# First rows of a scan kernel by products over 128 partitions, scaled by whole-tile operations

## The chip, the cores and the metric

The kernel runs on one core of a Trainium2 chip. The metric is the time of one execution on the device in microseconds (us); a kernel's time is the median of its runs. The profile is one further execution, recorded by the hardware profiler.

## The reference

The input x has 32 images of 48 channels, 64 rows and 128 columns in f32. Two layers of the same kind follow each other. A layer normalises x per image in 16 groups of 3 channels, scans the result in four directions, and adds what comes out to x:

```python
def step(w, b):
    def f(carry, inp):
        nxt = inp + _conv1d(carry, w, b)   # 5 taps, 48 channels to 48
        return (nxt, nxt)
    return f
...
# down over the rows, up over the rows, right over the columns, left over the columns
x = x + _L0_conv_ref(_gn(x), L0_conv_down_w, ...)
x = x + _L1_conv_ref(_gn(x), L1_conv_down_w, ...)
```

Each scan step needs the result of the step before it, so the steps form one chain: 63 steps down and 63 up, then 127 right and 127 left.

## The kernel before, in words

**Tiling.** The images are worked on in four groups of 8. For a scan over rows, a row of a group is a tile of three parts (o = 0 to 2) with 128 partitions and 128 columns each: eight neighbouring image columns e times 48 channels fill 3 x 128 partitions, and the 128 columns are 16 blocks k of such eight columns times 8 images b. The table PIECES says which channels of which e lie on which partitions of which part. A step is 9 matrix products (PRODUCTS, L856), each recorded as two instructions, and three vector operations (L865) that add the bias and the input row to the sums and write the new row. The phases (PHASES) are 8 row phases (4 groups, 2 layers) of 126 steps and 4 column phases of 254 steps, one after the other. TensorE works through this chain; all else is planned beside it.

**Order.** Instructions are put in an order written by hand: the function in_order ties every instruction to the one before it on its engine, so each engine works in the order of the program, and waits there. The calls at(t, ...) put other work into an agenda by step number; it is issued before that step. first_group is the start-up, which is issued in full before step 1 of the first phase; then the steps and the agenda alternate.

**The start-up before.** In the order of the program:

- load_kernel and make_ident load the small weights and build a selection matrix in the still unused tile of the later left weights (wleft); place_kernel has TensorE spread the weights over the partitions (L1210), and ACT copies them out (L1213, L1214).
- The first eight rows of the group go to a tile `top` in their natural layout, rows 0 to 3 on partitions 0 to 47 and rows 4 to 7 on partitions 64 to 111, by one load on SP's queue and one on ACT's. The whole group follows in `parts`: 16 loads of 768 KB on SP's queue, in a layout of 128 partitions that each hold 24 rows of input.
- DVE takes the statistics of the parts (L485, L488).
- put_rows permutes one of these 24 input rows by four copies (L637) on POOL or ACT into a tile, and put_out writes the tile to DRAM (`xin`) through SP's queue. All 24 must be there before every image row can be loaded back in the scan's layout.
- rows_by_product makes image rows 0 to 7 without the way through DRAM: a product with a piece of the selection matrix (48 partitions, 512 columns, L1243) moves the channels of one e to their partitions, reading `top` with a stride over the images, and ACT copies the sums out (L1250). Six such groups of products are needed (two sets of four rows, three parts): four come before the coefficients, two after.
- scaling computes scale and offset of each image and channel from the statistics through small products (L363, L374), a square root on ACT (L405) and small DVE operations (last is L415).
- scale_first scales rows 0 to 3, one image and part at a time: 15 operations on DVE (L711), 9 on ACT (L713). scale_rows does the same on ACT for the following rows (L688, 24 operations per call).
- move_rows loads image rows back from `xin`, ten loads (pieces) per call on SP's queue: rows 8 to 11, rows 12 to 15, and then eight at a time. ACT scales rows up to 47; scale_at_once does rows 48 to 63 on POOL with two whole-tile operations (multiply, then add; L699).

The copies need tiles that are still free: parts of the rows 8 to 31 of the scan's own tile, of the later weights, and of `stage`; a tile is used again when its write to DRAM has landed. The product tiles in PSUM (`rows0` to `rows2`) exist once each, so a group of products waits until ACT has copied the group before it out of the same tile.

Of the kernel before, what the change touches and what calls it, by code (L numbers as in the profile page):

```python
# [29 lines left out]
F32 = mybir.dt.float32  # L30
# [3 lines left out]
C = 48  # L34
# [7 lines left out]
GB = 8  # L42
# [77 lines left out]
def kernel(  # L120
# [62 lines left out]
    mask_in = wt["left"].rearrange("p i n -> p (i n)")[:, 5 * FULL : 5 * FULL + NG * C]  # L183
# [496 lines left out]
    def scale_rows(k, h0, h1):  # L680
        _, layer, g = PHASES[k]
        scale, offset = coeffs[layer, g]
        view = row_views(k)[h0 // HALF][:, :, h0 % HALF : h0 % HALF + h1 - h0]
        view = view.rearrange("p o h (k b) -> p o b h k", b=GB)
        for b in range(GB):
            for o in range(NG):
                args = view[:, o, b], scale[:, o, b : b + 1], offset[:, o, b : b + 1]
                nc.scalar.activation(  # L688
                    args[0], args[0], AF.Identity, bias=args[2], scale=args[1]
                )  # L690

    def scale_at_once(k, h0, h1, eng):

        _, layer, g = PHASES[k]
        view = row_views(k)[h0 // HALF][:, :, h0 % HALF : h0 % HALF + h1 - h0]
        view = view.rearrange("p o h (k b) -> p o (h k) b", b=GB)
        for t, op in zip(coeffs[layer, g], (ALU.mult, ALU.add)):
            t = t.unsqueeze(2).to_broadcast([FULL, NG, (h1 - h0) * NK, GB])
            eng.tensor_tensor(view, view, t, op)  # L699

    def scale_first(k, h1, split):

        _, layer, g = PHASES[k]
        scale, offset = coeffs[layer, g]
        view = row_views(k)[0][:, :, 0:h1].rearrange("p o h (k b) -> p o b h k", b=GB)
        for b in range(GB):
            for o in range(NG):
                it = view[:, o, b]
                by, on = scale[:, o, b : b + 1], offset[:, o, b : b + 1]
                if b < split:  # L710
                    nc.vector.tensor_scalar(it, it, by, on, ALU.mult, ALU.add)  # L711
                else:
                    nc.scalar.activation(it, it, AF.Identity, bias=on, scale=by)  # L713
# [431 lines left out]
    def first_group():  # L1145
# [6 lines left out]
        whole = shift[:, 0 : 2 * FULL + start - C // 3 + ODD]  # L1152
        part = shift[:, whole.shape[-1] : whole.shape[-1] + FULL + ODD]
        SETS = ((0, C), (ODD, ODD + C))

        def selects(piece, s=0):
            e, c0, c1, o, p0 = piece
            t, at = (part, 0) if c0 and p0 else (whole, start - p0 + c0)
            p, q = SETS[s]
            return t[p:q, at + p : at + p + FULL]  # L1160

        rows = PR // 2
        four = E8 // 2
        top = stage[:, 0:2].rearrange("p i n -> p (i n)").rearrange("p (b m) -> p b m", b=GB)
        parts = [wide_nat(SLOT + i * SLOT, rows) for i in range(2)]
        stats = InputStats("x0", GB)
        n = W * GB

        kernel = slot[slots(0)[0]][0:C, 0 : TAPS * C + 6]
        zeros = slot[slots(0)[0]][0:C, 512 : 512 + NG * FULL + 6]  # L1170

        def load_kernel():
            nc.vector.memset(zeros, 0.0)
            for j in range(TAPS):
                d, si = divmod(TAPS - 1 - j, 2)
                to = kernel[:, j * C : (j + 1) * C]
                dma(to, w[SIDES[si], 0, DOWN, d, SIDES[0]], nc.scalar if j % 2 else nc.sync)
            aside(kernel[:, TAPS * C :], bias[0:C].rearrange("c l k -> c (l k)"))

        def make_ident():  # L1180
            nc.vector.memset(shift[:, 0 : whole.shape[-1] + FULL + ODD], 0.0)
            for t, base in ((whole, start), (part, 2 * C - C // 3)):
                nc.gpsimd.affine_select(
                    t,
                    t,
                    pattern=[[1, t.shape[-1]]],
                    compare_op=ALU.not_equal,
                    fill=1.0,
                    base=-base,
                    channel_multiplier=-1,  # L1190
                )
            nc.gpsimd.memset(part[:, 0 : 2 * C], 0.0)
            nc.gpsimd.memset(part[:, 2 * C - C // 3 + ODD : 2 * C + ODD], 0.0)

        def place_kernel():
            for i in range(NG):
                ps = ps_rows.tile([FULL, BN], F32, tag=f"rows{i}", name=f"rows{i}")
                todo = [(selects(PIECES[0]), zeros, slice(0, NG * FULL + 6))]
                for piece in PIECES:
                    e, c0, c1, o, p0 = piece  # L1200
                    if o == i:
                        m = selects(piece)
                        for run in WEIGHT_RUNS:
                            if run[0:4] == (c0, c1, i, p0):
                                _, _, _, _, at, to, n = run
                                todo.append((m, kernel[:, at : at + n], slice(to, to + n)))
                        tail = slice(NG * FULL, NG * FULL + 6)
                        todo.append((m, kernel[:, TAPS * C :], tail))
                for j, (lhs, rhs, to) in enumerate(todo):
                    nc.tensor.matmul(  # L1210
                        ps[:, to], lhs, rhs, start=j == 0, stop=j == len(todo) - 1
                    )
                nc.scalar.copy(wt["down0"][:, i], ps[:, 0 : NG * FULL])  # L1213
                nc.scalar.copy(  # L1214
                    bd[:, i].rearrange("p l k -> p (l k)"), ps[:, NG * FULL :][:, 0:6]
                )

        free = [
            row_views(0)[0][:, o, h : h + 8].rearrange("p h n -> p (h n)")
            for h in (8, 16, 24)  # L1220
            for o in range(NG)
        ]
        free += [early[:, WEIGHTS + i * n : WEIGHTS + (i + 1) * n] for i in range(3)]
        free += [stage[:, i // 2, i % 2 * n : (i % 2 + 1) * n] for i in range(4, 8)]
        order = [*range(0, 4), *range(8, 12), *range(4, 8), *range(16, 20)]
        order += [*range(12, 16), *range(20, 24)]
        tiles = free + free[3:]
        put = [0]

        def put_rows(*engines):  # L1230
            for eng in engines:
                r, perm = order[put[0]], tiles[put[0]]
                put[0] += 1
                permute(parts[r // rows], r % rows, perm, (eng,))
                put_out(0, r, perm)

        def rows_by_product(s, o):
            src = top[SETS[s][0] : SETS[s][1]]
            src = src.rearrange("p b (r k e) -> p e r k b", k=NK, e=E8)
            ps = ps_rows.tile([FULL, four * N], F32, tag=f"rows{o}", name=f"rows{o}_{s}")  # L1240
            mine = [piece for piece in PIECES if piece[3] == o]
            for i, piece in enumerate(mine):
                nc.tensor.matmul(  # L1243
                    ps.rearrange("p (r k b) -> p r k b", r=four, b=GB),
# [4 lines left out]
                )  # L1249
            nc.scalar.copy(  # L1250
                row_views(0)[0][:, o, s * four : (s + 1) * four],
                ps.rearrange("p (r n) -> p r n", n=N),
            )

        pool, act = nc.gpsimd, nc.scalar
        load_kernel()
        for s, (p0, p1) in enumerate(SETS):
            src = x[0:GB].rearrange("b c h w -> c b (h w)")
            dma(
                top[p0:p1],  # L1260
                src[:, :, s * four * W : (s + 1) * four * W],
                nc.scalar if s else nc.sync,
            )
        for i in range(2):
            for b in range(GB):
                dma(parts[i][:, b], flat(b)[:, i * rows * W : (i + 1) * rows * W])
# [3 lines left out]
        place_kernel()  # L1270
        make_masks()
        for b in range(GB):
            stats.take(0, parts[0], b)
        put_rows(pool, act, pool, act)
        rows_by_product(0, 0)
        put_rows(pool, act, pool, act)
        rows_by_product(0, 1)
        put_rows(pool, act, pool)
        rows_by_product(0, 2)
        put_rows(pool)  # L1280
        rows_by_product(1, 0)
# [3 lines left out]
        put_rows(act, pool)  # L1285
        for _ in scaling("x0", 0, 0, stats, x_masks):
            pass
        scale_first(0, 4, 5)
        put_rows(pool, act, pool, act)
        rows_by_product(1, 1)  # L1290
        rows_by_product(1, 2)
        move_rows(0, 8, 12, False)
        put_rows(pool, act, pool, pool, pool, pool)
        move_rows(0, 12, 16, False)
        scale_rows(0, 4, 8)
        scale_rows(0, 8, 12)
        scale_rows(0, 12, 16)
        for h in range(16, 64, 8):
            move_rows(0, h, h + 8, False)
            if h < 40:  # L1300
                scale_rows(0, h, h + 8)
        take_in(1, 0, nats1[0])

    in_order(first_group)
    at(starts[0] + 10, scale_rows, 0, 40, 48)
# [72 lines left out]
```

## Time and profile before

| what | value |
|---|---|
| runs of the kernel (median of 3; lowest, highest) | 4215.19 us (4209.02, 4222.83) |
| the profiled execution's own time | 4228.38 us |
| its span, first to last instruction | 4226.6 us |
| coefficients ready (end of L415) | 50.9 us |
| first matmul of step 1 | 62.27 us |
| statistics (L485) begin, their last result (L488) begins | 12.41, 43.94 us |
| POOL's copies of rows begin and end (L637) | 25.7, 62.2 us |
| loads of rows 12 and on are issued from | 82.2 us |

Times in the tables and lines count from the first instruction. A line of the page's groups reads: source line, engine, operation, what it writes from what it reads, shapes, count, then the busy time and the mean duration of one in ns, and last the idle time of the engine just before it with what ended it. A line of the timeline reads: start, duration, engine, source line, operation, operands, count of merged instructions, and in brackets the idle time before it with its cause. PEld is TensorE's loading of a stationary matrix, which overlaps its products. Mean durations of single instructions overlap their neighbours; the spacing of a run of them is what they cost.

### The profile page before, as it was taken

To read this page: it belongs to the slowest core of one execution; us is meant where nothing else is said; L and a number is where in the kernel's file an instruction comes from. 1 tells how busy PE (TensorE), PEld (TensorE's weight loads), DVE (VectorE), ACT (ScalarE), POOL (GpSimd) and SP (SyncE) were. 2 spreads that over 40 slices of the span, in tenths; PEclk is the share of its full clock that TensorE was granted. 3 is DMA by queue.
4 is the path that set the end of the run, shared out by engine and by line. 5 is a ranking of instruction groups with operands and counts; after the bars stand their busy time and mean duration, and the time that the engine had idled before them with its cause. 6 is when DMAs were issued, how large, how long until landed. Compare 5 with 4: busy or idle time off the path is not lost. (4 is left out here: it accounts for less than half of the span.)

```text
span 4226.6 us, 90155 instructions
## 1 busy us (share of the span) xinstructions
PE 4086.4 (97%) x36724; PEld 4055.0 (96%) x36724; DVE 2135.8 (51%) x6501; ACT 1287.5 (30%) x2525; POOL 791.2 (19%) x737
## 2 busy tenths in 40 slices
PE   8999999999999999999999999999999999999992
PEld 6999999999999999989999999999999999999992
DVE  5454444456644454444457654444444444444443
ACT  6844000536874633000016854503000012110122
POOL 3520010334322100010023310000000034410352
PEclk9999999999999999999999999999999999999996
DMA  9987669659979997259419979759188059899999
GB/s 293 236 174 115 110 126 209 216 148 250 208 187 172 199 151 126 41 102 202 84 48 265 203 144 156 114 80 161 32 147 182 1 99 246 236 260 156 177 202 182
DMA packets 2118431, 680.55 MB, mean 161 GB/s; under 512 B 2006416, under 2 KB 2056832, under 8 KB 2079616
## 3 DMA queue, kind: packets, MB, share of 16 engines
q1 hardware_dynamic: 2015504, 582.07, 69.0%
q10 hardware_dynamic: 99952, 87.20, 9.7%
q0 software_dynamic: 2560, 5.51, 0.5%
q8 instruction: 289, 4.73, 0.5%
q14 instruction: 126, 1.03, 0.1%
HBM read 397.77 MB, written 295.14 MB: 164 GB/s over the span
## 5 line engine op out<-in xcount | busy, mean ns | idle before, releaser
L688 ACT ACTIVATE arena<-arena,offset,scale 128x256 f32<-128x256 f32 (+2 forms) x840 | 582.3, 788 | 310.4 <-DMA arena<-mid 176.8
L788 POOL TENSOR_TENSOR arena<-arena 128x2048 f32<-128x2048 f32 x80 | 362.9, 4548 | 1442.6 <-PE step_10l L856 461.4
L637 POOL COPY arena<-arena 128x256 f32<-128x256 f32 x332 | 196.7, 660 | 443.1 <-DMA arena<-in_x 394.2
L575 ACT ACTIVATE early<-arena 128x256 f32<-128x256 f32 x192 | 129.5, 674 | 453.6 <-DMA arena<-xin 315.2
L856 PE MATMUL step_01r<-arena,early 128*128 128x128 f32 x2286 | 254.2, 275 | 10.0 <-DMA arena<-arena 5.4
L856 PEld LDWEIGHTS step_01r<-arena,early 128*128 128x128 f32 x2286 | 253.3, 187 | 10.9 <-DVE arena L865 6.0
L856 PE MATMUL step_00r<-arena,early 128*128 128x128 f32 x2286 | 253.5, 275 | 8.7 <-DMA arena<-arena 4.4
L856 PEld LDWEIGHTS step_00r<-arena,early 128*128 128x128 f32 x2286 | 252.8, 186 | 9.4 <-issue 4.8
L856 PE MATMUL step_11r<-arena,early 128*128 128x128 f32 x2286 | 251.5, 274 | 5.5 <-DVE arena L865 5.5
L856 PEld LDWEIGHTS step_11r<-arena,early 128*128 128x128 f32 x2286 | 251.0, 185 | 5.9 <-DVE arena L865 5.8
L856 PE MATMUL step_00l<-arena,wleft 128*128 128x128 f32 x2286 | 249.3, 272 | 0.0
L856 PE MATMUL step_01l<-arena,wleft 128*128 128x128 f32 x2286 | 248.7, 272 | 0.1
L856 PEld LDWEIGHTS step_00l<-arena,wleft 128*128 128x128 f32 x2286 | 248.7, 184 | 0.0
L856 PEld LDWEIGHTS step_01l<-arena,wleft 128*128 128x128 f32 x2286 | 248.4, 184 | 0.3 <-DVE arena L865 0.3
L856 PE MATMUL step_10l<-arena,wleft 128*128 128x128 f32 x2286 | 248.5, 272 | 0.0
L856 PE MATMUL step_10r<-arena,early 128*128 128x128 f32 x2286 | 248.5, 272 | 0.0
L856 PE MATMUL step_11l<-arena,wleft 128*128 128x128 f32 x2286 | 248.5, 272 | 0.0
L856 PEld LDWEIGHTS step_10l<-arena,wleft 128*128 128x128 f32 x2286 | 248.4, 184 | 0.0
L856 PEld LDWEIGHTS step_10r<-arena,early 128*128 128x128 f32 x2286 | 248.4, 184 | 0.0
L856 PEld LDWEIGHTS step_11l<-arena,wleft 128*128 128x128 f32 x2286 | 248.4, 184 | 0.0
L813 ACT COPY arena<-arena 128x256 f32<-128x256 f32 x172 | 99.5, 655 | 409.0 <-POOL arena L788 154.1
L260 ACT COPY early<-arena 128x1 f32<-128x1 f32 x2 | 0.4, 192 | 655.0 <-DVE arena L865 655.0
(200 smaller groups left out, 7090.7 us busy)
## 6 DMA issues: line engine op xcount, KB each, us to landing
xin<-arena SPq DMA_DIRECT2D x91, 512.0 KB, 4.2
arena<-in_x SPq DMA_DIRECT2D x18, 2048.0 KB, 11.0
arena<-xin SPq DMA_DIRECT2D x96, 384.0 KB, 8.7
mid<-arena SPq DMA_DIRECT2D x96, 384.0 KB, 8.1
arena<-mid SPq DMA_DIRECT2D x192, 192.0 KB, 4.3
upb<-arena SPq DMA_DIRECT2D x192, 192.0 KB, 3.9
arena<-upb SPq DMA_DIRECT2D x96, 384.0 KB, 12.4
arena<-xin SPq DMA_DIRECT2D x180, 192.0 KB, 4.3
```

Source lines behind the costliest of these rows:

```text
L260: fn(*args)
L575: nc.scalar.activation(junk[:, 0:n], view[:, b], AF.Identity, accum_out=self.sum[:, i, j : j + 1])
L637: copy(dst[:, r, q], src[:, r0 + r, q])
L688: nc.scalar.activation(args[0], args[0], AF.Identity, bias=args[2], scale=args[1])
L788: eng.tensor_tensor(unit, unit, nat, ALU.add)
L813: copy(by_w(perm)[:, a], src[:, a])
L856: nc.tensor.matmul(part(whole(ps[o])[0:m], -s), weights[:, i, at : at + m], part(src(i), s), start=seen[o] == 1, stop=seen[o] == left[o],)
```

## The change

- `top` becomes a tile of 128 partitions in the scan's own row tile: rows 0 to 7 on partitions 0 to 47, rows 8 to 15 on partitions 64 to 111. The partitions in between are set to zero first (32 of them by POOL, 32 by DVE, 8192 elements each). Both loads are on SP's queue, behind the first load of the parts.
- Each of the eight tile rows of `top` is permuted on POOL or ACT in turn into `turned` (in `stage`), so that a product reads 32 neighbouring elements at a time.
- The selection matrix exists twice, each with zeros in the other set's partitions; every product, of the weights too, now uses 128 partitions. Image rows 0 to 15 come from products: 12 groups instead of 6, with 512 columns as before. Three groups come after the coefficients.
- place_kernel is split by part; the third part stands behind the first six groups.
- Rows 8 to 15 are no longer loaded back from `xin`. From row 16 on rows are loaded in calls of 4, 4 and then 8 rows.
- Rows 0 to 7 are scaled on DVE by scale_at_once, rows 0 to 3 before step 1, rows 4 and 5 in the agenda behind step 1, rows 6 and 7 behind step 3. Rows 8 to 15 are scaled by ACT as before; of rows 16 to 39 ACT scales part 0 and POOL parts 1 and 2 at once. scale_first goes away.
- The 24 input rows are put out in their order, 17 of them by POOL and 7 by ACT; the tiles are used in another order, among them `turned`. One small mask moves to another place (mask_in).

The diff, cut:

```diff
+    def scale_rows(k, h0, h1, groups=range(NG)):
+    def scale_at_once(k, h0, h1, eng, o0=0):
...
-    def scale_first(k, h1, split):
...
+            nc.vector.memset(kernel, 0.0)
+            nc.gpsimd.memset(top[2 * C // 3 : ODD], 0.0)
+            nc.vector.memset(top[2 * C : FULL], 0.0)
             nc.vector.memset(zeros, 0.0)
...
-        tiles = free + free[3:]
+        tiles = free[E8:] + free[E8 : E8 + 4] + free[0:4] + free[E8 : E8 + 1] + free[4:]
...
-        def rows_by_product(s, o):
-            src = top[SETS[s][0] : SETS[s][1]]
-            src = src.rearrange("p b (r k e) -> p e r k b", k=NK, e=E8)
+        def rows_by_product(s, r0, o):
+            src = turned[:, r0 : r0 + four].rearrange("p r (q e n) -> p e r q n", q=NQ, e=E8)
...
         load_kernel()
+        load_part(0, 0)
+        src = x[0:GB].rearrange("b c h w -> c b (h w)")
         for s, (p0, p1) in enumerate(SETS):
+            dma(top[p0:p1], src[:, :, s * E8 * W : (s + 1) * E8 * W])
+        for b in range(1, GB):
+            load_part(0, b)
+        for b in range(GB):
+            load_part(1, b)
...
         make_ident()
-        place_kernel()
+        place_kernel(0)
+        place_kernel(1)
         make_masks()
+        for r in range(E8):
+            permute(top, r, turned[:, r], ((pool, act)[r % 2],))
         for b in range(GB):
             stats.take(0, parts[0], b)
...
+        for o in range(NG):
+            rows_by_product(0, 0, o)
+            put_rows(pool)
+        for o in range(NG):
+            rows_by_product(0, four, o)
+            put_rows(pool, act)
+        place_kernel(2)
+        for o in range(NG):
+            rows_by_product(1, 0, o)
+            put_rows(pool if o % 2 else act)
         for b in range(GB):
             stats.take(NBN // 2, parts[1], b)
             stats.aggregate(b)
-        put_rows(act, pool)
+        put_rows(pool, act)
         for _ in scaling("x0", 0, 0, stats, x_masks):
             pass
-        scale_first(0, 4, 5)
-        put_rows(pool, act, pool, act)
-        rows_by_product(1, 1)
-        rows_by_product(1, 2)
-        move_rows(0, 8, 12, False)
-        put_rows(pool, act, pool, pool, pool, pool)
-        move_rows(0, 12, 16, False)
-        scale_rows(0, 4, 8)
+        put_rows(act)
+        scale_at_once(0, 0, 2, nc.vector)
+        scale_at_once(0, 2, 4, nc.vector)
+        put_rows(pool, pool)
+        for o in range(NG):
+            rows_by_product(1, four, o)
         scale_rows(0, 8, 12)
+        put_rows(pool, pool, pool, pool)
         scale_rows(0, 12, 16)
-        for h in range(16, 64, 8):
-            move_rows(0, h, h + 8, False)
+        put_rows(pool, pool, pool)
+        for h in (16, 20, 24, 32, 40, 48, 56):
+            end = h + (four if h < 24 else E8)
+            move_rows(0, h, end, False)
             if h < 40:
-                scale_rows(0, h, h + 8)
+                scale_rows(0, h, end, range(1))
+                scale_at_once(0, h, end, pool, 1)
         take_in(1, 0, nats1[0])
...
+    at(starts[0] + 1, scale_at_once, 0, 4, 6, nc.vector)
+    at(starts[0] + 3, scale_at_once, 0, 6, 8, nc.vector)
     at(starts[0] + 10, scale_rows, 0, 40, 48)
```

## The prediction

> **What bounds the kernel now.** I read the page first, then the timeline of the first 120 us, the stretches (busy time by window), and the groups of instructions by shape.
>
> ```profile
> PE 4086.4 (97%) x36724; PEld 4055.0 (96%) x36724; DVE 2135.8 (51%) x6501; ACT 1287.5 (30%) x2525; POOL 791.2 (19%) x737
> ```
>
> TensorE is busy 97% of the span, in one chain of dependent steps. The diff touches only what happens before the chain runs freely, so two moments count: when step 1 starts, and how much the next twenty steps lose. From the timeline:
>
> ```profile
> 22.88 20.54 PE L1243 MATMUL rows<-arena,wleft 48*128 48x512 f32 x26
> ...
> 49.23 13.10 PE L1243 MATMUL rows<-arena,wleft 48*128 48x512 f32 x14
> ...
> 50.45 0.43 DVE L415 TENSOR_SCALAR offset<-offset 128x24 f32<-128x24 f32 x1
> ...
> 62.27 10.94 PE L856 MATMUL step_00d<-arena,early 128*128 128x128 f32 x72
> ...
> 97.66 0.35 DVE L865 SCALAR_TENSOR_TENSOR arena<-step_00d,bd,arena 128x128 f32<-128x128 f32 x1 [6.83 <-DMA arena<-xin]
> ...
> 111.05 0.35 DVE L865 SCALAR_TENSOR_TENSOR arena<-step_00d,bd,arena 128x128 f32<-128x128 f32 x1 [4.22 <-ACT arena L688]
> ...
> 119.20 0.61 DVE L865 SCALAR_TENSOR_TENSOR arena<-step_00d,bd,arena 128x128 f32<-128x128 f32 x2 [0.73 <-PE step_00d L856]
> ```
>
> The coefficients are ready at 50.9, but step 1 starts at 62.27, behind the last two products of the rows (49.23 to 62.3). A free step takes 1.975 us (L865's single lines at 69.29 and 71.27), and its first L865 comes 1.17 us after its first matmul (75.01, 76.18). The line at 119.20 is step 19. Unhindered it would stand at 62.27 + 18 x 1.975 + 1.17 = 99.0, so **20.2 us** are lost: row 12 came late from DRAM, row 16 waited for ACT's scaling, the rest is small waits and a slow clock. Afterwards the steps run at 1.975. The sum to beat is 62.3 + 20.2 = **82.5**.
>
> The clock needs care. Stretches, TensorE alone:
>
> ```profile
> 23.00:33.00 10.00, 10.00 (x12) 1.00 1.02 420
> ...
> 62.30:66.20 3.90, 3.90 (x19) 1.00 0.96 283
> 68.20:72.10 3.90, 3.90 (x38) 1.00 0.95 187
> ```
>
> The third column is the granted clock. It says 1.00 throughout, but the same 128-row matmuls come twice as densely after 68 us. So until 68 TensorE ran at half speed and the column merely had no record. The 48-row products start 0.91 us apart (weight loads at 23.93, 24.85, 25.76), as slow in their last stretch as in their first.
>
> **The change, part by part.** Durations, first 160 us by shape:
>
> ```profile
> L1243 PE MATMUL rows<-arena,wleft 48*128 48x512 f32 x40 | 33.6, 1099 | 0.0
> L485 DVE BATCH_NORM_STATS2 bn_x<-arena 128x6 f32<-128x512 f32 x48 | 29.6, 673 | 10.2 <-DMA arena<-in_x 10.2
> L637 POOL COPY arena<-arena 128x256 f32<-128x256 f32 x44 | 26.0, 639 | 20.6 <-DMA arena<-in_x 19.3 <-DMA xin<-arena 1.3
> L699 POOL TENSOR_TENSOR arena<-arena,scale 128x3072 f32<-128x3072 f32 x1 | 6.7, 6711 | 89.6 <-DVE arena L865 89.6
> L1181 DVE MEMSET wleft<- 128x608 f32 x1 | 0.6, 565 | 0.1
> ```
>
> *New memsets.* DVE and POOL each clear 32 partitions of 8192 elements. 608 elements took DVE 0.565 us and 128 took 0.165 (0.83 ns each); 1152 took POOL 1.06 and 96 took 0.18 (0.84). So **6.9 us each**, side by side, done near 8. The two loads of the first rows wait for them, and behind those on SP's queue all further input loads. DVE then clears zeros (0.4) and the selection matrix (832 elements, 0.75) until 9.2; POOL builds one set in about 1.3 us. TensorE can start placing weights at 10.6 instead of 2.63.
>
> *Input.* The first rows are now 3.1 MB instead of 1.6. At 350 GB/s (between 296 in the first 20 us with 2 KB pieces and 415 from 20 to 40 us with 6 KB pieces; these are 4 KB) that is 9 us; with 2.1 us of latency (the small weight loads) they land near 19. The other fifteen loads (768 KB at 415 GB/s: 1.9 us) end near 47 instead of 41, so L485's statistics end near 50 instead of 44. TensorE, below, hides this.
>
> *Placing weights.* Before: 20.4 us for three parts. First part at half speed 5.6 (2.63 to 8.19): 16.2. Second at full speed, half of its 7: 19.7. ACT copies it out: 20.4.
>
> *Turning the first rows*: 32 new copies, half on POOL (20 took 11.75: 2.35 us a row), half on ACT (8 took 4.55: 2.3 a row). ACT starts only after the weight copy at 20.4: rows 1 and 3 at 25.0, all at 29.6. POOL's share runs 19 to 28.
>
> *Products.* 40 matmuls instead of 20, so 80 instructions instead of 40. The trace has no 128-row product of 512 columns. Dearest end: 0.91 each as now, 73 us in all. Cheapest: a step's matmul takes 1.975/18 = 0.11 us for 128 columns at full speed, times four 0.44, 35 us in all. I take 0.44: every 128-row stretch in this trace reached full speed within 4 to 6 us (62.27 to 68; resumed 98.1, full at 102), the 48-row ones never. [...] So the first three cost 6 x 0.91 + 14 x 0.44 = 11.7: 25.0 to **36.7**. The next three 8.8: 45.5. The third part of the weights, now behind them, 3.3: 48.8. Rows 8 to 11, 8.8: **57.6**. ACT's copies out (0.5 each) and permutes in between fit.
>
> *Coefficients.* Their first matmul stands behind these products, at 57.6 instead of 44.4. Their square root stands on ACT behind one copy out and the copies of two rows (0.5 + 2 x 2.3): 62.7. Offset 3.3 later as now (47.61 to 50.88): 66.0. TensorE goes on at 64.2, after the mean.
>
> *Last products* (rows 12 to 15): TensorE did almost nothing for 6 us, so slow again, 11.7: **75.9**. Step 1 starts there. DVE's four whole-tile operations on rows 0 to 3 (128x768; a 128x2048 took DVE 2.29 at best, so 0.9 each, 3.6) are hidden until then; without that cover they would cost 3.6.
>
> *DVE inside the scan.* Two pairs, behind steps 1 and 3: 1.8 us, of which the 0.7 idle before L865 is free. Queued behind them are that step's three L865, for which TensorE waits. [...] POOL then copies rows at 0.59 each. By the idle time alone 1.1 a pair, less 0.5 by which L865 runs ahead[...]. I take 1.0: **2.0** together. Bounds 1 and 3.6.
>
> *Rows 8 to 15 without DRAM.* Away go 20 load issues on SP and the waits at rows 8 and 12. ACT scales them (24 x 0.39 = 9.4 us for four rows): rows 8 to 11 by 86, rows 12 to 15 by 95.5; needed at 92 and 100.
>
> *Rows 16 on.* The copies of input rows 17 to 20 reuse tiles that the last products read, so POOL resumes at 75.9: seven rows x 2.35 = 92.4. SP's loads of rows 16 to 19 stand behind: issued 92.5 to 97.5 (now 82.2 to 86.9), landed 100, then POOL scales two thirds (2 x 1024 elements at 2.18 ns, 4.5 us): 104.5. Needed at 75.9 + 15 x 1.975 + 1.2 + 2 = 108.7. Row 24: loads 10.5 us for eight rows, landed 115, POOL 9.0: 124; needed 124.5. So no stall, but row 24 is tight; unknown 0 to 4.
>
> **Sum.** 75.9 + 2.0 = 77.9 against 82.5: **4.6 us less**. The profiled execution (span 4226.6, its own time 4228.4) would become 4223.8; it lay 13.2 above the median 4215.2 of the runs, which becomes **4210.6**, say 4211. The bill: 20.2 us of late rows and slow clock removed, 13.6 given back as a later step 1, 2.0 as DVE's stalls.
>
> **Rivals.**
> *The 128-row products stay at half speed* (half their rows multiply zeros). Placing ends at 24, products start at 29.3, the chain reaches 91, step 1 at 116 and begins slow: 116 + 2 + 2 - 82.5 = +37, **4252**. For it: 20 us of gapless 48-row work never woke the clock. Against: each 128-row stretch did. It decides if the spacing is still 0.9 after the first six instructions. Chance 0.10.
> *The clock stays full* in both gaps, as the small matmuls count: 2 x 2.5 to 3 less, **4205**; with no DVE stall 4202. For it: waits under 2 us at steps 4 and 8 did not slow it. Chance 0.20.
> *The start is later*: loads after the memsets slower than 350 GB/s, or row 24 stalls because the last seven copies wait for the last products. 4 to 12 us more, about **4218**. The 0.5 us of slack speaks for it. Chance 0.20.
> Likeliest case: 0.50.
>
> **The numbers.** 0.3% of 4215 is 12.6, about what a measurement of this kernel can tell from no change. Faster than that: half of the full-clock case and a little of the likeliest, 0.12. Slower: the half-speed case and the worse part of the late one, 0.18. Within: 0.70. The range 4199 to 4234 leaves out 0.08 below and 0.12 above.
>
> **What would show it.** Product instructions 0.44 apart but for the first six or so; step 1 near 76 and later than 62; no wait on xin in L865 before row 16; first coefficient matmul near 58 with the statistics done by 50. Wrong if the copies of the first rows begin well after 20, or L865 waits for rows 16 to 24.

## The result and the profile after

The changed kernel takes 4243.59 us (median of 4 runs, 4241.56 to 4245.67), the kernel before 4214.57 us (median of 4). The ratio on record is 1.0055, with a 95% interval of 1.0037 to 1.0073: it is **slower by 0.55%**, some 23 us (16 to 31). The two medians alone lie 29.0 us apart, which is inside that interval. The forecast was 4211 us, the range 4199 to 4234. The profiled execution spans 4243.9 us, 17.3 more than that of before.

In the lines of the profile PE is TensorE, DVE is VectorE, ACT is ScalarE, POOL is GpSimd and SP is SyncE. The page's first line, busy time of each engine, hardly moves: TensorE is 8 us less busy in 17 us more of span, so the loss is waiting.

```profile
PE 4078.3 (96%) x36764; PEld 4047.8 (95%) x36764; DVE 2138.8 (50%) x6496; ACT 1260.6 (30%) x2466; POOL 844.5 (20%) x774
```

The timeline of the changed kernel shows where step 1 went:

```profile
0.80 6.92 POOL L1161 MEMSET arena<- 32x8192 f32 x1 [0.29 <-POOLq L1368]
...
2.95 6.88 DVE L1162 MEMSET arena<- 32x8192 f32 x1 [1.76 <-issue]
...
33.29 9.35 POOL L637 COPY arena<-arena 128x256 f32<-128x256 f32 x16 [15.82 <-DMA arena<-in_x]
33.31 8.91 ACT L637 COPY arena<-arena 128x256 f32<-128x256 f32 x16 [8.81 <-issue]
...
38.05 19.52 PE L1231 MATMUL rows<-arena,wleft 128*128 128x512 f32 x40 [14.13 <-POOL arena L637]
...
70.83 0.28 PE L363 MATMUL ps_x<-mv_x_x,mask_x 128*128 128x8 f32 x2
...
77.15 11.85 PE L1231 MATMUL rows<-arena,wleft 128*128 128x512 f32 x20
88.84 4.11 PE L842 MATMUL step_00d<-arena,early 128*128 128x128 f32 x36
```

GpSimd waits 15.82 us for the load of the first rows and starts its copies at 33.3; TensorE then waits 14.13 us for those copies. Step 1 starts at **88.84**; it was 62.27 before, and 75.9 in the forecast. The line of bytes moved in the first 40 us, one number per microsecond in GB/s, of the kernel before and then of the changed one, says why:

```profile
GB/s 0 11 33 116 283 287 272 291 311 268 270 424 424 412 412 430 418 412 412 430 418 412 406 436 418 412 406 430 424 406 412 430 424 412 406 424 436 399 412 387
```

```profile
GB/s 0 0 34 105 197 375 123 0 66 229 143 127 135 152 123 119 127 135 131 127 156 168 127 119 147 135 127 131 127 135 137 133 184 418 418 424 406 418 424 424
```

Before, two loads of the first rows run together (4 to 10 us) at 270 to 310 GB/s; then the parts come at 415. Now, from 10 to 32 us, the two loads run one after the other at about **134 GB/s**, though the 16 DMA engines are as busy as ever (the "DMA share" of the stretch 10 to 20 us is 1.03). So each packet takes longer: the 768 packets of 4 KB took 484 ns each on average.

The second loss is in the scan:

```profile
89.07 19.45 POOL L637 COPY arena<-arena 128x256 f32<-128x256 f32 x28 [11.02 <-PE rows L1231]
...
109.09 74.93 SPq L249 DMA_DIRECT2D arena<-xin  x70
...
135.70 4.54 POOL L699 TENSOR_TENSOR arena<-arena,scale 128x2048 f32<-128x2048 f32 x1 [6.42 <-DMA arena<-xin]
140.32 4.52 POOL L699 TENSOR_TENSOR arena<-arena,offset 128x2048 f32<-128x2048 f32 x1
144.88 0.61 DVE L851 SCALAR_TENSOR_TENSOR arena<-step_00d,bd,arena 128x128 f32<-128x128 f32 x2 [5.34 <-POOL arena L699]
```

The last seven copied rows wait for the last products, so that the first of 70 row loads is issued at 109.09; rows 24 to 31 land at 135.7, GpSimd has scaled them at 144.84, and VectorE waits 5.34 us for it in step 24. The granted clock of TensorE is 0.50 behind that pause, from 144.7 to 151.5.

Since the steps that follow are the same, the end of each step (the last of its three vector operations, L865 before and L851 in the changed kernel), set against the same step of the kernel before's profiled execution, is a ruler of some 0.1 us. All kernels of this study, us later (+) or earlier (-) than before; the last column compares with the kernel before in the same session (its median was 4220.17 us for the four e kernels):

| kernel | step 1 | step 8 | step 20 | step 26 | step 64 | time against before (95%) |
|---|---|---|---|---|---|---|
| changed | +24.5 | +23.4 | +10.1 | +18.4 | +20.4 | 1.0055 (1.0037 to 1.0073) |
| e1_two_queues | +29.6 | +28.5 | +15.1 | +21.7 | +27.8 | 1.0052 (1.0035 to 1.0069) |
| e2_spread_partitions | +12.6 | +11.5 | -1.6 | +6.2 | +10.7 | 4235.8 us, one run |
| e3_before_one_queue | +5.5 | +5.3 | +4.5 | +4.5 | +4.5 | 1.0010 (1.0001 to 1.0019) |
| e4_products_48_rows | +59.4 | +58.4 | +44.4 | +49.8 | +55.9 | 4283.1 us, one run |
| b1_one_wide_load | +87.1 | +86.0 | +72.4 | +81.1 | +86.3 | 1.0190 (1.0173 to 1.0207) |
| b2_wide_load_and_order | +86.4 | +85.3 | +71.3 | +71.3 | +77.1 | 1.0188 (1.0174 to 1.0202) |
| b3_order_alone | +34.5 | +36.3 | +22.3 | +22.3 | +22.0 | 1.0029 (1.0018 to 1.0039) |
| b4_products_first | +93.6 | +91.4 | +77.3 | +77.3 | +77.1 | 1.0170 (1.0156 to 1.0184) |
| c3_order_and_negate | +23.6 | +29.1 | +15.1 | +15.1 | +14.8 | 1.0035 (1.0022 to 1.0048) |
| c1_interleaved_load | +9.4 | +8.2 | -5.2 | +2.5 | +9.7 | 1.0020 (1.0011 to 1.0029) |
| c2_interleaved_order_negate | +19.2 | +20.8 | +6.8 | +6.8 | +6.5 | 1.0006 (0.9996 to 1.0016) |
| c4_products_first | +6.7 | +5.5 | -8.5 | -7.2 | +1.9 | 1.0005 (0.9995 to 1.0016) |
| d1_copies_shared | +7.0 | +5.3 | -8.8 | -8.8 | -6.9 | 0.9980 (0.9972 to 0.9988) |
| d2_and_row_48_split | +7.0 | +5.3 | -8.7 | -8.7 | -9.0 | 0.9981 (0.9972 to 0.9989) |

A row of this table that falls from step 8 to step 20 shows the gain that the change does bring: at 1.975 us a step these twelve take 23.7 us, and the kernel before needs 37.7 (row 12 comes late from DRAM, row 16 waits for ScalarE's scaling), the changed one 24.4. Behind step 64 the profiled executions drift against each other by up to 14 us (e3 from +4.5 to -9.8), for which no cause was found. So the ruler says where the time was lost, and the ratios how much.

### The profile page after: what moved, and what is told of

It reads as the page before. It is cut to its first block, busy times and chain, and to the rows that moved or that the text cites. A ratio compares the mean times of both kernels' runs of the same rounds, so it can differ in the third digit from the quotient of the medians.

```text
span 4243.9 us, 90167 instructions
## 1 busy us (share of the span) xinstructions
PE 4078.3 (96%) x36764; PEld 4047.8 (95%) x36764; DVE 2138.8 (50%) x6496; ACT 1260.6 (30%) x2466; POOL 844.5 (20%) x774
## 5 line engine op out<-in xcount | busy, mean ns | idle before, releaser
L688 ACT ACTIVATE arena<-arena,offset,scale 128x256 f32<-128x256 f32 (+2 forms) x776 | 551.4, 804 | 360.1 <-DVE arena L851 139.4
L637 POOL COPY arena<-arena 128x256 f32<-128x256 f32 x368 | 220.5, 659 | 466.6 <-DMA arena<-in_x 418.4
```

The costliest lines, as they stand in the source:

```text
L637: copy(dst[:, r, q], src[:, r0 + r, q])
L688: nc.scalar.activation(args[0], args[0], AF.Identity, bias=args[2], scale=args[1])
```

## The experiments

**First four: the late load.** The theory (H) was that a load which writes 48 partitions of one half runs at a third of the speed (134 of some 415 GB/s); the rivals, that the pieces it reads are slow (S), or that a late load costs nothing in the end. e1 puts the second half of the first rows on ACT's queue; e2 reads the same pieces of DRAM but writes them over all 128 partitions (the first 16 rows then hold other data, and GpSimd has two small fills more); e3 takes the kernel before and puts both its loads of the first rows on one queue; e4 uses only the 48 filled rows in each product.

```diff
 e1     dma(top[p0:p1], src[:, :, s * E8 * W : (s + 1) * E8 * W],
+           nc.scalar if s else nc.sync)
 e2     piece = src[:, s * E8 * W : (s + 1) * E8 * W]
+       dma(top[:, 3 * s : 3 * s + 3], piece.rearrange("(p i) n -> p i n", p=FULL))
 e3 (kernel before)
-       nc.scalar if s else nc.sync,
+       nc.sync,
 e4     selects(piece, s)[SETS[s][0] : SETS[s][1]], src[SETS[s][0] : SETS[s][1], piece[0]]
```

> The changed kernel, with the second half of the first rows (partitions 64 to 111) loaded on ACT's queue instead of SP's, so that both halves are in flight at once. Theory H (halves: a load that writes only one half of the partitions gets some 135 GB/s, two at once on both halves 270): 3.1 MB land 11.6 us after about 10, at 22 instead of 33; step 1 starts about 11 us earlier than in the changed kernel, near 78 instead of 88.8, and the time falls by about 11 to near 4232. Theory S (source: pieces of 4 KB that lie 32 KB apart in DRAM come slowly, whatever they are written to): landing stays near 33, step 1 near 88, the time near 4243. Row 24 keeps its wait of about 5 us in both.

> The changed kernel, both loads still one after the other on SP's queue and with the same pieces of DRAM (384 rows of 4 KB, 32 KB apart, per load), but written over all 128 partitions, three pieces on each. The first 16 image rows then hold other data than the reference's; the work is the same except for two small memsets. Theory H: the loads move at 270 to 400 GB/s, 3.1 MB land 8 to 12 us after about 10, at 18 to 22. Theory S: 134 GB/s as in the changed kernel, landing near 33. A theory that one queue alone is slow expects 33 as well.

> The kernel before, with its second load of the first rows (partitions 64 to 111, pieces of 2 KB) on SP's queue instead of ACT's. Theory H: two loads of 0.79 MB one after the other at 135 GB/s take 11.6 us instead of about 7 together, so the first part of the statistics' input lands 4 to 5 us later than 12.4 and the coefficients come 4 to 5 us later than 50.9; step 1 starts up to 5 us later. Theory S: the rate of the kernel before, some 275 GB/s, has nothing to do with two queues, and nothing moves by more than 1 us.

> The changed kernel, with products of the first rows that use only the 48 partitions of their set, weights and moving rows, still reading 32 neighbouring elements at a time. If it is the number of rows that keeps TensorE's clock low, the 80 instructions are 0.85 to 0.91 us apart throughout and step 1 starts some 30 us later than 88.8, near 119. If it was the strided reading that made the products of the kernel before slow, they are 0.43 apart after the first 5 us and step 1 stays near 89.

e2 decides between H and S. Bytes moved, 0 to 40 us:

```profile
GB/s 0 0 35 86 184 406 123 0 0 0 0 74 295 422 414 434 410 438 401 442 406 418 430 418 406 418 430 418 406 424 424 418 399 430 418 424 399 432 424 406
```

The same pieces, read on the same single queue, now come at 420 GB/s, a packet of 4 KB in 159 ns (median); the copies begin at 21.1, right behind GpSimd's fills, and step 1 at 76.91, one microsecond from the forecast's 75.9. So neither the size of the pieces nor the single queue is the cause, and the late load is worth 12 us at step 1 and as much at step 26 (+6.2 instead of +18.4). e3 shows the same from the other side: with the two loads of the kernel before on one queue, the statistics, whose first part is loaded behind them, begin at 17.64 instead of 12.41, about as much later as theory H's 135 GB/s for each load gives (4 to 5 us), and step 1 comes 5.5 us later; 4.5 us of that stay.

One rival is left. e2 changes the partitions and, with them, the order in which the pieces are read: in the changed kernel the next piece of a partition is the same channel of the next image, in e2 it is the neighbouring channel. No run changes the order alone. Against it stands the kernel before, which reads in the changed kernel's order and still moves 270 to 310 GB/s while both halves are in flight. That the written partitions set the speed is therefore likely, not proved; that this layout of the load does is shown.

e1 should have given the two halves together. It didn't: ACT issued its load at 9.87, but from 11 to 21 us only 123 to 147 GB/s moved, as with one half-load alone in the changed kernel (134); from 21 to 37 us it was 190 to 264, parts included, and ACT's load landed 27.9 us after its issue. Step 1 came 5 us later still. Why ACT's load added nothing before 21 us is open.

TensorE's timeline of e4:

```profile
39.71 32.63 PE L1231 MATMUL rows<-arena,wleft 48*128 48x512 f32 x38
...
80.38 17.43 PE L1231 MATMUL rows<-arena,wleft 48*128 48x512 f32 x20
...
121.66 6.68 PE L842 MATMUL step_00d<-arena,early 128*128 128x128 f32 x36
```

The products stay 0.86 us apart from first to last (20 in 17.43 us, where 128 rows take 8.83). Two stretches of TensorE (the window, its length, busy time with the count of products, granted clock, DMA share and GB/s) show the clock itself:

```profile
38.00:72.00 34.00, 34.00 (x40) 0.50 0.96 375
73.00:80.40 7.40, 7.39 (x31) 0.50 0.35 119
```

The reading is contiguous in e4 and in the changed kernel, and the edit touches nothing but the rows of these products, so it is the number of rows that leaves their clock at half, not the stride. It isn't the whole rule: the second stretch holds the third part of the weights, products of 128 rows and 390 columns, and the clock stays at 0.50 there too. The change's step to 128 rows is right and worth about 33 us at step 1 (121.7 against 88.8).

**Three kernels with a wide load, a miss.** They read each image's first rows by one load over 128 partitions. The partitions 48 to 63 and 112 to 127 then hold the next channels, and here these also enter the sums, so that the first 16 rows hold other data.

```diff
-       for s, (p0, p1) in enumerate(SETS):
-           dma(top[p0:p1], src[:, :, s * E8 * W : (s + 1) * E8 * W])
+       for b in range(GB):
+           piece = src[b * C : b * C + ODD, 0 : 2 * E8 * W]
+           dma(top[:, b], piece.rearrange("c (s n) -> s c n", s=2))
```

> The changed kernel, with the first rows read by eight loads (one an image) that write all 128 partitions: the lower half gets rows 0 to 7, the upper half rows 8 to 15, and partitions 48 to 63 and 112 to 127 take the next 16 channels in place of zeros, so that both fills of 32 partitions (6.9 us each) go too. 4.2 MB instead of 3.1. Theory A (the late first step is the cost of a load that writes one half of the partitions, and the delay stays in the total): 4 KB packets near 160 ns and 420 GB/s, the rows landed by 17 us instead of 33.3, step 1 near 73 instead of 88.8, the time 14 us under the changed kernel's, near 4229, with the wait at row 24 still there. Rival B (steps 8 to 23 are paced by the loads of rows written out, whatever step 1 does, as when the kernel before got its first step 5.5 us later and lost only 0.1%): step 1 as early, but the time within 4 us of the changed kernel's.

> As the run with the wide loads, and the last eight write-outs of permuted rows go through the row buffers of rows 16 to 31 and the two early ones again instead of the tiles that the last products read. Theory A: no wait for the last products ahead of those copies, rows 24 to 31 scaled in time, no stall at row 24: 8 us less again, near 4221. Rival B: the row 24 stall only moves to another wait (the loads of rows written out, at rows 16 to 32), and 3 us or less come of it.

> As the run with wide loads and the other order of tiles, and the products of rows 12 to 15 come ahead of the coefficients, the third placing of weights ahead of the first products: TensorE then has no 2 to 6 us pauses and half clock between 58 and 77, and the square root no copies ahead of it. Theory A: step 1 near 67 instead of 73 and 6 us less again, near 4215, at best level with the kernel before: all of the change's loss would then come from where its loads and waits were put. Rival B: what is won ahead of step 1 is lost at rows 8 to 16 as waits for evictions or scaling, the time within 3 us of the run with wide loads and order.

All three came 86 to 94 us later than the kernel before at step 1. The stretches of b1, by columns: the window, its length, busy time of TensorE, weight load, VectorE, ScalarE and GpSimd with their counts, the granted clock, the DMA share and GB/s:

```profile
10.00:20.00 10.00, 4.97 (x28) 4.42 (x26) 0.00 (x0) 0.54 (x2) 0.00 (x0) 0.81 0.13 53
20.00:40.00 20.00, 0.00 (x0) 0.00 (x0) 0.00 (x0) 0.00 (x0) 0.00 (x0) 0.50 0.13 53
```

A DMA share of 0.13 is two engines of 16. They move 53 GB/s, by which a packet of 4 KB takes some 155 ns (an estimate from these two numbers), as quick as in e2 (159 ns). The slowest dimension of this load's access is the pair of halves, two long; in c1 below, where it is 64 channels, the DMA share of 10 to 20 us is 1.03, with 418 GB/s. That the one comes of the other is not shown: c1 puts the channels on other partitions too. These runs tell nothing of the theory, and one thing of the order of tiles: b2 and b4 have no loss from step 20 to 26, b1 loses 8.7.

**The order of tiles alone.** In the changed kernel the last copied rows use the tiles that the last products read. b3 lets them go through other tiles a second time.

```diff
-       tiles = free[E8:] + free[E8 : E8 + 4] + free[0:4] + free[E8 : E8 + 1] + free[4:]
+       tiles = free[E8:] + free[E8 : E8 + 4] + free[0:4] + free[E8:]
```

> The changed kernel with the other order of tiles alone, its loads as they were. Theory A: step 1 stays near 88.8; VectorE's wait of 5.3 us for GpSimd's scaling at row 24 and the half clock behind it go: 8 us less, near 4235. Rival B: the copies wait for the landing of their tiles' earlier write-outs, or GpSimd is still late because VectorE's scaling slows its copies: 3 us or less.

The loss of 8.3 us from step 20 to 26 is gone (+22.3 at both), as theory A has it. But step 1 comes 10 us later, which neither theory had. The timeline:

```profile
78.56 11.64 POOL L637 COPY arena<-arena 128x256 f32<-128x256 f32 x20
...
79.29 15.53 DVE L415 TENSOR_SCALAR offset<-offset 128x24 f32<-128x24 f32 x1
...
90.10 4.68 POOL L637 COPY early<-arena 128x256 f32<-128x256 f32 x8
```

L415, the last small step of the coefficients, takes 15.53 us. It ends at 94.82, when GpSimd's unbroken train of copies ends (94.78). In the changed kernel, where GpSimd stands idle at that time, it takes 0.18:

```profile
78.45 0.18 DVE L415 TENSOR_SCALAR offset<-offset 128x24 f32<-128x24 f32 x1
```

The wait for the last products, which I wanted to remove, had kept GpSimd quiet while VectorE finished the coefficients and scaled the first rows.

**The same with L415 reading PSUM.**

```diff
-       nc.vector.tensor_tensor(offset, mean, scale, ALU.mult)
-       nc.vector.tensor_scalar(offset, offset, -1.0, None, ALU.mult)
+       nc.vector.tensor_tensor(mean, mean, scale, ALU.mult)
+       nc.vector.tensor_scalar(offset, mean, -1.0, None, ALU.mult)
```

> The changed kernel with the other order of tiles, and the last step of the coefficients (the negation, L415) reading PSUM instead of SBUF. In the run with the order alone that one operation of 128x24 took 15.53 us instead of 0.18, from 79.3 until GpSimd's 32 gapless copies ended at 94.8. Theory A (a VectorE operation with one SBUF source[...] waits as long as GpSimd's copies follow each other without a gap; row 24's stall is the copies' wait for the last products): L415 near 0.2 us, VectorE's scaling of the first rows 1.3 to 1.45 each instead of 0.95 but done before the products end at 88.8, step 1 level with the changed kernel's, no wait at row 24, the scan 8.3 us ahead of the changed kernel's from step 26 on. Rival B (the copies hold VectorE back whatever it runs): the next operations, with two SBUF sources, take the 15 us instead, step 1 near 97 again.

Half right. L415 takes 0.18 again and step 1 is level with the changed kernel's; step 26 is 3.3 us ahead of it, not 8.3, as one of VectorE's scalings behind step 1 now took 7.00 us, again until GpSimd's train ended. In c2 below it was the first scaling, with two SBUF sources. The timeline of c2:

```profile
56.49 18.53 POOL L637 COPY arena<-arena 128x256 f32<-128x256 f32 x32 [2.29 <-PE rows L1228]
...
64.26 16.18 DVE L699 TENSOR_TENSOR arena<-arena,scale 128x768 f32<-128x768 f32 x1
...
74.96 4.66 POOL L637 COPY early<-arena 128x256 f32<-128x256 f32 x8
...
80.47 0.96 DVE L699 TENSOR_TENSOR arena<-arena,offset 128x768 f32<-128x768 f32 x1
```

So rival B was right in part: either kind of operation can be held. GpSimd's copies meanwhile run at their own 0.58 us. In other runs (b2's four scalings, c4 below) the two take turns instead, VectorE at 1.2 to 1.45 and GpSimd, in c4, at 0.77 a copy. c3 has both beside one train of 40 copies (70.38 to 96.54): four scalings of 1.19 to 1.38 us before step 1, then the one of 7.00. What decides between turns and holding out is open.

**The load interleaved.** Channel c's two halves go to partitions 2c and 2c+1, so that the slowest dimension is the 64 channels; the selection matrices step by two, their rows from 96 on are zero, and the two fills go.

```diff
+           dma(top[:, b], piece.rearrange("c (s n) -> c s n", s=2))
...
-                to = kernel[0:C, j * C : (j + 1) * C]
+                to = kernel[0 : 2 * C : 2, j * C : (j + 1) * C]
...
-                        pattern=[[1, t.shape[-1]]],
+                        pattern=[[2, t.shape[-1]]],
...
-                        base=p0 - base,
+                        base=s - 2 * base,
```

> The changed kernel with the first rows read by eight loads (one an image) whose slowest dimension is the channel: channel c's rows 0 to 7 on partition 2c, its rows 8 to 15 on partition 2c+1, 64 channels of which the last 16 meet zero rows of the selections; the weights are loaded to every second partition, the selection matrices have a step of two, and both 6.9 us fills are gone. The earlier wide loads had the two halves as slowest dimension and ran at 26 GB/s, on 2 of the 16 DMA engines. Theory A (what made the first step late is that a load writes one half of the partitions): 4 KB packets at 159 ns and 420 GB/s, the rows landed near 17 instead of 33.3, GpSimd's and ScalarE's copies from there, step 1 15 us ahead of the changed kernel's, its wait of 8 us at row 24 unchanged, the time near 0.4% under the changed kernel's, level with the kernel before. Rival B (an earlier step 1 is given back later): step 1 so early, but the scan under 5 us ahead from step 26 on.

(The 26 GB/s in that text is the share of one engine; the two together moved 53.) Bytes moved by c1, 0 to 40 us:

```profile
GB/s 0 0 12 29 111 240 401 410 344 418 414 414 418 426 414 414 418 418 436 412 412 412 430 418 412 412 424 424 412 412 424 424 418 406 430 420 412 399 442 403
```

And of its timeline:

```profile
18.47 9.34 POOL L637 COPY arena<-arena 128x256 f32<-128x256 f32 x16 [9.84 <-DMA arena<-in_x]
...
73.65 4.11 PE L842 MATMUL step_00d<-arena,early 128*128 128x128 f32 x36
```

Copies from 18.5, step 1 at 73.65: 15.2 us ahead of the changed kernel, and 15.8 at step 26, where its own loss at row 24 (7.8 us) is about that of the changed kernel (8.3). Theory A holds to there; the time falls from 1.0055 to 1.0020, and does not reach the kernel before. From step 26 to 64 it loses another 7.2 us, where the changed kernel lost 2.0: at row 48 VectorE waits 6.1 us for GpSimd's scaling (3.2 in the changed kernel), and GpSimd had waited for that row's load. The earlier the steps, the more they run into the rows' loads.

**All together**, then with the products of rows 12 to 15 ahead of the coefficients:

```diff
 c4     place_kernel(1)
+       place_kernel(2)
...
+       for o in range(NG):
+           rows_by_product(1, four, o)
        put_rows(pool, act)
        for _ in scaling("x0", 0, 0, stats, x_masks):
```

> Interleaved load, the other order of tiles and the negation from PSUM together. Theory A: the gains add, 16 + 8 us ahead of the changed kernel's scan from step 26 on, so some 6 us ahead of the kernel before: 0.15% faster than that one. Rival B: with step 1 earlier the loads of rows 16 to 24 come too late, 5 us or more of it lost there.

> As the one before, with the third placing of weights ahead of the first products and the products of rows 12 to 15 ahead of the coefficients, so that TensorE has no 6 us with almost nothing to do and no half clock in its last 20 products, and the square root has no copies ahead of it. Theory A: 6 us ahead of the one before from step 26 on, 12 us ahead of the kernel before: 0.3% faster than it. Rival B: what is won before step 1 is lost at rows 8 to 24.

c2 lost what it won: its 16.18 us of held scaling put step 1 at +19.2. c4 had the turns, step 1 at 69.3 and the best scan so far at step 20 (-8.5), and then gave back 10.4 us until step 64: its copies ended at 85.3 (24.6 us for eight rows) and the 70 loads began at 86.28.

**The last copies shared.** d1 gives ScalarE four of the last ten rows; d2 also has ScalarE scale a third of rows 48 to 55.

```diff
 d1
-       put_rows(act)
+       put_rows(act, pool, act, pool, act, pool, act)
...
-       put_rows(pool, pool)
-       put_rows(pool, pool, pool, pool)
+       put_rows(pool, pool, pool)
...
-       put_rows(pool, pool, pool)
 d2
+    at(starts[0] + 12, scale_rows, 0, 48, 56, range(1))
-    at(starts[0] + 26, scale_at_once, 0, 48, 56, nc.gpsimd)
+    at(starts[0] + 26, scale_at_once, 0, 48, 56, nc.gpsimd, 1)
```

> As the run with the products ahead of the coefficients, but of the last ten rows copied, ScalarE takes four and GpSimd six (it was one and nine). Theory A (the last write-out of a permuted row paces all later rows: behind it SyncE issues 70 loads, 1.07 us each, at whose end GpSimd scales rows 48 to 55 for 13.4 us): GpSimd's copies end near 77 instead of 85.3, the first of the 70 loads is issued near 79 instead of 86.3, the small waits at row 24 go and the wait at row 48 shrinks from 6 to 8 us to near nothing: the scan 7 to 8 us under the kernel before at step 64, where it was 1.9 over it. Rival B (it is the share of the loads themselves, or the later scaling by GpSimd): the loads earlier, the waits at rows 24 to 48 within 2 us of what they were.

> As the one before, and of rows 48 to 55 ScalarE scales the first third of the channels, so that GpSimd needs 9 us instead of 13.4. Theory A: no wait left from step 12 to 64, the scan 8.5 us under the kernel before at step 64, the time 0.2 to 0.3% under that kernel's. Rival B: ScalarE's scaling delays the next group's input (its statistics start at 173) and as much is lost at the start of the second phase.

SyncE's loads of rows, in d1:

```profile
78.83 77.89 SPq L249 DMA_DIRECT2D arena<-xin  x70
```

And VectorE's one wait for rows behind step 20:

```profile
170.02 0.87 DVE L851 SCALAR_TENSOR_TENSOR arena<-step_00d,bd,arena 128x128 f32<-128x128 f32 x3 [3.06 <-POOL arena L699]
```

The loads begin 7.5 us earlier than in c4, and nothing is lost from step 20 to 40 (-8.8); at row 48 VectorE waits 3.1 us instead of 6.3. d2 removes that too (-9.0 at step 64). Both theories A hold. Both kernels are **faster than the kernel before, by 0.2%** (0.9980, 0.9972 to 0.9988, and 0.9981, 0.9972 to 0.9989); they can't be told apart from each other.

## Why the prediction was wrong, point by point

- **Fills and placing.** Right in size: 6.92 and 6.88 us. VectorE's began at 2.95, behind a small fill and a wait, so the identity was ready at 12.6 instead of 10.6. It cost the changed kernel nothing, as the load came later still; in e2 ScalarE, behind its copy of the weights, began on the rows at 21.8 instead of 20.4, which is about e2's last microsecond.
- **Input: the step that failed.** "At 350 GB/s (between 296 in the first 20 us with 2 KB pieces and 415 from 20 to 40 us with 6 KB pieces; these are 4 KB) that is 9 us; with 2.1 us of latency ... they land near 19." They landed at 33.3, at 134 GB/s: the term of 9 us measured 23. I took the speed from the size of the pieces; it depended on how the load lies over the partitions. Both my bounds came from stretches in which both halves were being written, by two queues or by loads of 128 partitions, and the change took away just that: it put both half-loads on one queue. What one half-load moves alone, the trace of before did not show; but half of the 270 to 310 GB/s that two moved together would have been an estimate for this term, 20 to 23 us for 3.1 MB. e2 and c1, with the load over all partitions, take the delay away, and e3 brings it into the kernel before; only the order of reading, which e2 and c1 change too, was not tested alone. Step 1 moved by 12.9 us for it (88.84 against 75.9).
- **Turning the rows, products, coefficients, last products.** Right. Four rows took 9.35 and 8.91 us (2.34 and 2.23 each); the first products 0.85 apart until 42.4, then 0.43; the square root waited behind ScalarE's copies (3.04 us); the last 20 took 11.85 (11.7 forecast), the first six slow. From the start of ScalarE's copies (33.31) to step 1 it took 55.5 us, in the forecast 75.9 - 20.4 = 55.5.
- **DVE inside the scan.** From VectorE's timeline of the changed kernel:

```profile
91.28 1.02 DVE L699 TENSOR_TENSOR arena<-arena,scale 128x768 f32<-128x768 f32 x1
92.34 1.30 DVE L699 TENSOR_TENSOR arena<-arena,offset 128x768 f32<-128x768 f32 x1
...
96.53 1.35 DVE L699 TENSOR_TENSOR arena<-arena,scale 128x768 f32<-128x768 f32 x1
97.91 1.28 DVE L699 TENSOR_TENSOR arena<-arena,offset 128x768 f32<-128x768 f32 x1
```

  2.0 forecast; steps 2 to 5 took 3.05, 2.20, 3.36 and 2.20 instead of 1.975, 2.9 more. L699 took 0.95 alone (at 78.54, with GpSimd idle) and up to 1.35 beside GpSimd's copies.
- **Rows 8 to 15 without DRAM.** Right: no waits at rows 8 and 12; 14.5 us of the head start of before were made good from step 1 to 20.
- **Rows 16 on: the second step that failed.** "So no stall, but row 24 is tight; unknown 0 to 4." It cost 8.3. The loads were issued 20.3 us behind step 1 instead of 16.6, as GpSimd's copies beside VectorE took 19.45 us for seven rows (2.78 each, not 2.35), and rows 24 to 31 landed 26.6 us behind the first issue instead of 22.5: 7.8 us, less the 0.5 of slack and the later steps in between, leaves roughly the wait of 5.34. The half clock behind the wait, which was not in the sum, is 3 us more. The cause is the wait of those copies for the last products: b2 differs from b1 only in the tiles of its last copies, its step 1 comes within 0.7 us of b1's, and it loses nothing from step 20 to 26 where b1 loses 8.7.
- **The sum.** -4.6 forecast, + 12.9 (load) + 8.3 (row 24) + 0.9 (DVE) = +17.5; the ruler shows +18.4 at step 26 and +20.4 at step 64, and the runs +16 to +31.
- **The rivals.** "The start is later" named both mechanisms, with 4 to 12 us and a chance of 0.20. Both happened, and together were 21: the direction was seen, the size was not. The half speed of 128-row products did not come (e4 shows what it would have cost); nor did the clock stay full in the gaps (granted 0.50 from 26 to 42 and from 77 to 83, as it was in the kernel before from 98 to 102, behind a pause of 5.65 us).

What the change removed was real: 14.5 us from step 1 to 20. It was paid for by a step 1 that was to come 13.6 us later and came 26.6 us later, and by 8.3 us at row 24. With the load over 128 partitions and without the two fills, other tiles for the last copies, L415 reading PSUM, the products ahead of the coefficients and the copies shared, the kernel is 0.2% faster than before (d1, d2). No run shows what each of these parts is worth in that total.

## What to carry to other kernels

Before a transfer is costed by its bytes, look at which partitions it writes, and in a trace at how many engines carry it: the same 3.1 MB took some 9 us (e2) or 23 (the changed kernel), and at a DMA share of 0.13 (b1) 53 GB/s was all that came. When a wait is removed, ask whom it kept quiet: GpSimd's idle 11 us were what let VectorE finish in 0.18 us what then took 15.5. And follow a queue to its end: here the last copied row sets when 70 loads start, and all rows behind.

## What the runs showed of the hardware that was not expected

- One load into 48 partitions of one half: 134 GB/s; two such loads into the two halves on two queues, in the kernel before: 270 to 310. The two can overlap, then, but in e1, with the second issued at 9.87, no more than 147 GB/s moved from 11 to 21 us.
- A VectorE operation with SBUF sources was held until a whole train of GpSimd's copies ended, for 15.53 (b3), 16.18 (c2) or 7.00 us (c3), not only for one copy (0.58 us). In c4 the first four scalings took turns with it, at 1.21 to 1.39 us.
- 48-row products of 512 columns ran at half clock for 32.6 us without a gap (e4, 38 in a row at 0.86, granted clock 0.50); those of 128 rows in the changed kernel woke within 4.3 us (38.05 to 42.4). But 30 products of 128 rows and 390 columns ran through 7.4 us of e4 (73.0 to 80.4) at 0.50, where the same ones take 3.95 us at full clock in the changed kernel.
